# Moving the pooling work to other places in the queues of an attention loop

## The chip, the cores and the metric

The kernel runs on one core of a Trainium2 chip. The metric is device time in microseconds (us) of the whole program. The engines of the core are TensorE (PE in the profile; its weight loads are PEld), VectorE (DVE), ScalarE (ACT), GpSimd (POOL) and SyncE (SP, which issues most transfers). Each has its own queue of instructions, and they wait for each other through semaphores.

## The reference

The input is four images of 128 channels and 64 x 64 points. Layer 0 is a group norm, three 1x1 convolutions and full attention over the 4096 points of an image. Layer 1 takes the points as tokens. It has two parts, each with a residual addition: a causal attention with running maximum and running sums over 8 heads, and a sparse expert layer, which the change concerns:

```
logits = einsum('bsd,ed->bse', x, gate_w) + gate_b       # 64 experts
probs  = softmax(logits, axis=1)                          # over the 4096 tokens
vals, idx = top_k(probs.transpose(0, 2, 1), 8)            # 8 tokens for each expert
gathered  = take x at idx
pooled    = einsum('bked,bke->bed', gathered, topv)       # weighted sum of those 8
out       = two dense layers per expert on pooled
outputs[idx] += out * topv
```

"Pooling" below is the way from the logits to `pooled`: for every expert find the eight largest logits among 4096 tokens, take their probabilities, set all others to zero, and multiply by the tokens.

## The kernel before

Layer 0 fills the first 1500 us or so. Then comes the loop over 32 blocks n of 512 tokens (8 blocks for each of the four images; function `loop`, L977 to L1037), in which attention runs one block ahead of the gate, and after it the experts.

In a block PE works in this order, which is written out by hand (`manual_schedule` for PE, L1039): the keys of block n + 1 for the first four heads (`pk`, L687), the turned exponentials of block n (`pe`, L769), the turned gate tokens (`gtr`, L888), the keys of the other four heads, the values (`pv`, L805), the gate's logits (`pl`, L896), the turned tokens of block n + 2 (`ltr`, L677), the totals (`pt`, L821), the scores of block n + 1 (`ps`, L706) and the outputs (`po`, L841 and L848). Most of these results go through one ring of three PSUM buffers (tag `kv`). So a matmul into it waits until the result of three places before has been read: a key by its Silu on ScalarE (`ks`, L689), a value by its Silu (`v`, L809), `gtr` and `ltr` by copies on ScalarE (L890, L679).

The scores go through `scan`: VectorE makes a running maximum (`mm`, L723) and a difference (`ss`, L727); ScalarE takes its Exp (L728); VectorE makes running sums (`rr`, L738) and their reciprocal (L743); GpSimd copies the exponentials (`es`, L733). `spread` sends `rr` through memory to all partitions (`rb`, L751 and L758), and `weighted` multiplies `em` by `rb` on VectorE (L793). The scan of block n + 1 is written in block n, ahead of `outputs`.

Pooling of the first two images (group p = 0) is woven into the loop. With k0 = n - 18:

- `select(0)`, in block 18: finds the eight largest of the candidates (`cand`, eight for each 512 tokens) and marks the rest so that they match nothing.
- `pick(0, k0)`, in blocks 18 to 25: the **mark** (L927, VectorE) writes `left`, a copy of 512 logits with the chosen ones replaced by the lowest number; the **Exp** (L930, ScalarE) overwrites the logits with their exponentials and sums them up; the **choice** (L933, VectorE) keeps those whose place in `left` is the lowest number and sets the rest to zero.
- `pick_turn(0, k0 - 1)`, in blocks 19 to 26: four transposes (`ctr`, L940, between the keys and the values) and a multiplication (`ct`, L943, VectorE).
- `pick_add(0, k0 - 1)`, in the same blocks: 32 small matmuls (`pp`, L955, between the logits and `ltr`) and an addition (L967).
- `divisors(0)`, in block 26: sums and a reciprocal.

The two other images (p = 1) go through the same functions after the loop.

On engines other than PE, a planner sorts the instructions by their place in the program and by when it reckons their data to be ready. `tc.issue_after(i)` around some code adds an edge: instructions of that code on the engine of i come later in the queue than i. Before the change the pooling of block n is written behind `scan(n + 1)` with two such edges:

```
made = scan(n + 1, score(n + 1, ks))
rbs = spread(n + 1, made[1])
with tc.issue_after(made[2][0]), tc.issue_after(made[2][1]):
    if k0 == 0:
        select(0)
    if 0 <= k0 < NBLK:
        pick(0, k0)
```

`made[2][0]` is the scan's Exp and `made[2][1]` the reciprocal. So pooling's Exp is behind the scan's Exp, and mark and choice are behind the reciprocal.

ScalarE loads a table whenever it goes over from one of Exp, Silu and Sqrt to another (ACT_TABLE_LOAD in the profile; the gate's norm has a Sqrt, L90).

Of the kernel before, what the change touches and what calls it, by code (L numbers as in the profile page):

```python
# [8 lines left out]
F32 = mybir.dt.float32  # L9
AF = mybir.ActivationFunctionType  # L10
ALU = mybir.AluOpType
AX = mybir.AxisListType
PSUM = bass.MemoryType.PSUM
P = 128
LOWEST = -3.4028234663852886e38
# [3 lines left out]
def conv_attn_hybrid_kernel(  # L19
# [22 lines left out]
    nc = tc.nc  # L42
# [7 lines left out]
    BLK = 512  # L50
    NBLK = N // BLK
# [258 lines left out]
    with ExitStack() as l0:  # L310
# [36 lines left out]
        aas = load("aas", [P, 1], (every[:1], aa.to_broadcast([P, 1])))  # L347
# [289 lines left out]
    def layer1(pre, ready):  # L637

        with ExitStack() as kept, ExitStack() as l1:
            pool = opener(kept, pre)  # L640
            lgp = pool("lg", side="right")
            gp = pool("gate", side="right")
# [6 lines left out]
            ps_kv = pool("l1kv", 3, space=PSUM)  # L649
# [13 lines left out]
            def tokens(n):  # L663
# [6 lines left out]
                    made.append(xl)  # L670
                return made + [last]

            def turned(n, xls):

                ptr = ps_kv.tile([P, NPAIR, 2, 2, H2], F32, tag="kv", name=f"{pre}ltr_{n}")
                for c, xl in enumerate(xls[:CPB]):
                    nc.tensor.transpose(ptr[:, c // 2, :, c % 2, :], xl, ident)  # L677
                xt = sb.tile([P, BLK], F32, tag="xt", name=f"{pre}xt_{n}", bufs=3)
                nc.scalar.copy(xt, ptr.rearrange("p q s u j -> p (q s u j)"))  # L679
                return xt  # L680

            def keys(n, xt, heads):
# [19 lines left out]
            def score(n, ks):  # L702
                pss = ps_s.tile([P, BLK], F32, tag="s", name=f"{pre}ps_{n}")
                for h in range(NH):
                    g, r = h % QG, h // QG
                    nc.tensor.matmul(  # L706
                        pss[g * QW : (g + 1) * QW, :], qz[:, h, :], ks[h],
                        start=(r == 0), stop=(r == NR - 1),
                    )
                return pss  # L710
# [80 lines left out]
            def weighted(ems, rbs):  # L791
                for em, rb in zip(ems, rbs):
                    nc.vector.tensor_mul(em, em, rb.rearrange("p s h j -> p (s h) j"))  # L793
                return [em.rearrange("p (s h) j -> p s h j", s=2) for em in ems]
# [67 lines left out]
            rden = lgp.tile([P, B // 2], F32, tag="rden", name=f"{pre}rden")  # L862

            total = lgp.tile([P, B // 2, C + 1], F32, tag="total", name=f"{pre}total")
            gmv, grs, xgs, xts, picks, cts = {}, {}, {}, {}, {}, {}

            def gate_stats(n):
                gmv[n] = gp.tile([P, CPB, 2], F32, tag="gmv", name=f"{pre}gmv_{n}", bufs=2)
# [34 lines left out]
            def select(p):  # L903

                flat = cand[p].rearrange("p k e -> p (k e)")
                top = gp.tile([P, 8], F32, tag="top", name=f"{pre}top_{p}")
                nc.vector.max(out=top, in_=flat)
                ng = gp.tile([P, 1], F32, tag="ng", name=f"{pre}ng_{p}")
                nc.vector.tensor_scalar_mul(ng, top[:, 0:1], -1.0)
                sel = gp.tile([P, NBLK * 8], F32, tag="sel", name=f"{pre}sel_{p}")  # L910
                nc.vector.match_replace(
                    out=sel, in_to_replace=top, in_values=flat, imm_value=-LOWEST
                )
                nc.vector.tensor_scalar(
                    out=sel, in0=sel, scalar1=1e38, scalar2=None, op0=ALU.is_ge
                )
                nc.vector.tensor_mul(flat, flat, sel)
                nc.vector.tensor_scalar(
                    out=sel, in0=sel, scalar1=1.0, scalar2=3e38, op0=ALU.subtract, op1=ALU.mult
                )  # L920
                nc.vector.tensor_add(flat, flat, sel)
                picks[p] = ng

            def pick(p, k):
                lg = lgs[p][:, bass.ts(k, BLK)]
                left = gp.tile([P, BLK], F32, tag="left", name=f"{pre}left_{p}_{k}")
                nc.vector.match_replace(  # L927
                    out=left, in_to_replace=cand[p][:, k, :], in_values=lg, imm_value=LOWEST
                )
                nc.scalar.activation(  # L930
                    lg, lg, AF.Exp, bias=picks[p], accum_out=den[:, p, k : k + 1]
                )
                nc.vector.scalar_tensor_tensor(  # L933
                    out=lg, in0=left, scalar=-3.3e38, in1=lg, op0=ALU.is_le, op1=ALU.mult
                )

            def pick_turn(p, k, ps):
                ptr = ps.tile([P, CPB, P], F32, tag="kv", name=f"{pre}ctr_{p}_{k}")
                for c in range(CPB):
                    nc.tensor.transpose(ptr[:, c, :], lgs[p][:, bass.ts(k * CPB + c, P)], ident)  # L940
                ct = gp.tile([P, CPB, 2, E], F32, tag="ct", name=f"{pre}ct_{p}_{k}", bufs=2)
                rs = rs1[:, bass.ts(p, 2 * NCH)].rearrange("t (z i) -> t i z", z=2)
                i = nc.vector.tensor_mul(  # L943
                    ct, ptr.rearrange("t c (z e) -> t c z e", z=2),
                    rs[:, bass.ts(k, CPB), :].unsqueeze(3).to_broadcast([P, CPB, 2, E]),
                )
                cts[p, k] = ct
                return i.ins
# [20 lines left out]
            def divisors(p):  # L969
                nc.vector.tensor_reduce(rden[:, p : p + 1], den[:, p, :], AX.X, ALU.add)  # L970
                nc.vector.reciprocal(rden[:, p : p + 1], rden[:, p : p + 1])
# [5 lines left out]
            def loop():  # L977
                xt = {n: turned(n, tokens(n)) for n in range(2)}
                made = scan(0, score(0, keys(0, xt[0], range(NH))))
                rbs = spread(0, made[1])  # L980
                for n in range(NB):
                    more = n + 1 < NB
                    if more:
                        ks = keys(n + 1, xt[n + 1], range(NH // 2))
                    if n >= 1:
                        gate_stats(n - 1)
                    if not more:
                        gate_norm(n - 1, nc.vector)
                    if n + 2 < NB:
                        xls = tokens(n + 2)  # L990
                    if n == 0:
                        ks += keys(n + 1, xt[n + 1], range(NH // 2, NH))
                    es, rr, _ = made
                    ems = weights(n, es)
                    if n >= 2:
                        gate_turn(n - 2, ps_kv)
                    if more and n > 0:
                        ks += keys(n + 1, xt[n + 1], range(NH // 2, NH))
                    k0 = n - (B // 2 * NBLK + 2)
                    if 1 <= k0 <= NBLK:  # L1000
                        with tc.issue_after(pick_turn(0, k0 - 1, ps_kv)):
                            aas = weighted(ems, rbs)
                    else:
                        aas = weighted(ems, rbs)
                    vs, last = values(n, xt[n])
                    if n >= 2:
                        best = gate_logits(n - 2, ps_kv)
                    if not more:
                        gate_turn(n - 1, ps_kv)
                    if 1 <= k0 <= NBLK:  # L1010
                        pick_add(0, k0 - 1)
                    with tc.issue_after(last):
                        if n >= 1 and more:
                            gate_norm(n - 1, nc.gpsimd)
                        if n == 0 and ready:
                            roots(rs1[:, bass.ts(B - 1, NCH)], mv1[:, bass.ts(B - 1, NCH), :])
                    if n + 2 < NB:
                        xt[n + 2] = turned(n + 2, xls)
                    totals(n, vs)
                    if not more:  # L1020
                        best()
                        best = gate_logits(n - 1, ps_kv)
                    if more:
                        made = scan(n + 1, score(n + 1, ks))
                        rbs = spread(n + 1, made[1])
                        with tc.issue_after(made[2][0]), tc.issue_after(made[2][1]):
                            if k0 == 0:
                                select(0)
                            if 0 <= k0 < NBLK:
                                pick(0, k0)  # L1030
                            if k0 == NBLK:
                                divisors(0)
                    outputs(n, rr, aas, vs)
                    if n >= 2:
                        best()
                    if n == 0 and ready:
                        test_rows(gp, ps_kv)  # L1037
# [118 lines left out]
            for g in range(EG):  # L1156
# [5 lines left out]
                p, k = g // NBLK, g % NBLK  # L1162
# [100 lines left out]
```

## Time and profile before

| what | value |
|---|---|
| time, median of 3 | 2557.14 us (2555.38 to 2559.95) |
| span of the profiled execution | 2555.8 us |
| PE / DVE / ACT / POOL busy | 94% / 66% / 47% / 12% |
| the chain that ended last | PE 84%, DVE 9%, ACT 3%, DMA 2% |
| attention loop, first and last key or output matmul | 1501.4 to 2390.5 us |
| the scan's reciprocal (L743) | 32 times 3353 ns |
| mark (L927), Exp (L930), choice (L933) | 670, 722, 658 ns in the loop |
| table loads | 1283 ns each: 32 for the scan's Exp (L728), 40 for the keys' Silu (L689), 33 for the Sqrt (L90) |

The page's busy shares are means over stages of different kinds. What a change in one stage is worth has to be read from the blocks of that stage: how long a block is, how much of it PE is busy, and what ends PE's waits. The granted clock (PEclk) is the share of full speed at which PE ran. A wait for several semaphores is put down to the one that came last.

### The profile page before, as it was taken

How to read it: one execution, taken by the hardware profiler on the slowest of the kernel's cores; microseconds unless marked ns; L12 is line 12 of the kernel's file. 1: busy time of each engine (PE TensorE's matmuls, PEld its weight loads, DVE VectorE, ACT ScalarE, POOL GpSimd, SP SyncE). 2: the span in 40 equal slices, each digit the busy share in tenths (PEclk: the TensorE clock that was granted, in tenths of full speed). 3: DMA queues.
4: the chain of work that ended last, by engine and by line, in shares of the span. 5: the costliest groups of instructions: out<-in, count | busy, mean ns of one | idle time of the engine just before them, and what ended most of it. 6: DMA issues, size and time to landing. Idle time of an engine off the chain costs nothing.

```text
span 2555.8 us, 45522 instructions
## 1 busy us (share of the span) xinstructions
PE 2412.5 (94%) x19348; PEld 1598.9 (63%) x19348; DVE 1677.5 (66%) x2648; ACT 1206.8 (47%) x1575; POOL 310.0 (12%) x370
## 2 busy tenths in 40 slices
PE   5899999999999999999999989999999888899787
PEld 3567767677677677776777755555555454555543
DVE  6777777777776777766666656666666655566524
ACT  2344434444344444444444445666666555566341
POOL 0000000000000000000000003333333332333100
PEclk9999999999999999999999999999999889999898
DMA  3100110000100000000000001212212110112485
GB/s 97 54 17 16 26 47 9 17 13 22 50 13 5 21 17 17 17 9 9 5 9 5 5 18 35 52 38 49 51 36 52 35 35 19 34 36 51 157 330 209
DMA packets 48292, 111.03 MB, mean 43 GB/s; under 512 B 10192, under 2 KB 19024, under 8 KB 47952
## 3 DMA queue, kind: packets, MB, share of 16 engines
q1 hardware_dynamic: 46784, 107.77, 14.3%
q8 instruction: 153, 2.51, 0.4%
q14 instruction: 59, 0.48, 0.1%
q10 hardware_dynamic: 1296, 0.26, 0.1%
HBM read 86.38 MB, written 8.91 MB: 37 GB/s over the span
## 4 chain that ended last, share of the span: by engine, by line
PE 84%; DVE 9%; ACT 3%; DMA 2%; issue 1%; SPq 0%; ACTq 0%; DVEq 0%
PE av L494 33%; PE sc L470 17%; PE pv L805 8%; PE pk L687 8%; PE po L841 3%; PE pt L821 2%; DVE rr L743 2%; PE ps L706 1%; PE pa L437 1%; PE ph L1108 1%; PE pd L519 1%; DVE before L831 1%; PE pp L955 1%; PE pe L415 1%; PE pl L896 1%
## 5 line engine op out<-in xcount | busy, mean ns | idle before, releaser
L494 PE MATMUL av<-pr,am 64*128 64x512 f32 x4096 | 1189.6, 592 | 5.2 <-DVE o L505 5.2
L474 ACT ACTIVATE pr<-sc 128x1024 f32<-128x1024 f32 x512 | 523.9, 1023 | 704.4 <-PE sc L470 692.3
L494 PEld LDWEIGHTS av<-pr,am 64*128 64x128 f32 x4096 | 679.2, 188 | 257.9 <-issue 59.0
L481 DVE TENSOR_TENSOR acc<-acc,pr 128x1024 f32<-128x1024 f32 x480 | 585.5, 1220 | 332.3 <-ACT pr L474 320.2
L470 PE MATMUL sc<-e,e 64*128 64x512 f32 x2048 | 736.8, 594 | 0.0
L470 PEld LDWEIGHTS sc<-e,e 64*128 64x128 f32 x2048 | 351.7, 188 | 101.9 <-issue 28.8
L687 PE MATMUL pk<-xt,wks 128*128 128x512 f32 x512 | 252.3, 634 | 13.4 <-ACT ks L689 9.0
L805 PE MATMUL pv<-wvs,xt 128*128 128x512 f32 x512 | 227.7, 598 | 2.6 <-ACT v L809 2.6
L809 ACT ACTIVATE v<-pv 128x512 f32<-128x512 f32 x256 | 152.6, 597 | 71.4 <-PE pv L805 71.4
L687 PEld LDWEIGHTS pk<-xt,wks 128*128 128x128 f32 x512 | 96.2, 202 | 127.1 <-issue 81.4
L689 ACT ACTIVATE ks<-pk 128x512 f32<-128x512 f32 x256 | 146.8, 597 | 60.0 <-PE pk L687 59.6
L805 PEld LDWEIGHTS pv<-wvs,xt 128*128 128x128 f32 x512 | 97.4, 192 | 122.0 <-issue 115.4
L793 DVE TENSOR_TENSOR em<-em,rb 128x1024 f32<-128x1024 f32 x64 | 78.3, 1234 | 139.1 <-DMA rb<-rd 138.9
L695 POOL MEMSET ew<- 128x1024 f32 x1 | 1.0, 952 | 1050.6 <-PE pa L437 1050.6
L841 PEld LDWEIGHTS po<-v,em 64*64 64x64 f32 x4096 | 111.4, 133 | 26.7 <-DVE before L831 26.7
L95 POOL TENSOR_SCALAR xg<-t,gmv,grs 128x128 f32<-128x128 f32 x120 | 94.6, 801 | 237.4 <-DVE grs L91 122.8
L784 POOL TENSOR_TENSOR em<-et,mask 128x1024 f32<-128x1024 f32 x64 | 120.3, 1901 | 22.6 <-ACT et L771 22.6
L728 ACT ACT_TABLE_LOAD x32 | 41.1, 1283 | 169.5 <-DVE ss L727 169.5
L841 PE MATMUL po<-v,em 64*64 64x128 f32 x4096 | 119.2, 271 | 0.0
L527 DVE RECIPROCAL den<-den 128x512 f32<-128x512 f32 x32 | 107.3, 3353 | 1.1
L743 DVE RECIPROCAL rr<-rr 128x512 f32<-128x512 f32 x32 | 107.3, 3353 | 1.1
L729 POOL COPY state<-mm 128x1 f32<-128x1 f32 x32 | 20.6, 644 | 511.8 <-DVE mm L723 511.8
(164 smaller groups left out, 2319.1 us busy)
## 6 DMA issues: line engine op xcount, KB each, us to landing
rb<-rd SPq DMA_DIRECT2D x128, 256.0 KB
fw<-in_fw_dram SPq DMA_DIRECT2D x64, 512.0 KB
x<-in_x_dram SPq DMA_DIRECT2D x16, 512.0 KB
xr<-in_x_dram SPq DMA_DIRECT2D x32, 256.0 KB
e<-ee SPq DMA_DIRECT2D x64, 128.0 KB
out_dram<-t SPq DMA_DIRECT2D x16, 512.0 KB
e<-ee SPq DMA_DIRECT2D x64, 64.0 KB
rd<-rr SPq DMA_DIRECT2D x64, 8.0 KB
```

Of the source, the lines that this page charges most:

```text
L470: nc.tensor.matmul(sc[:, u, :], e2[halves[u], p, :], e1[halves[u], :], start=True, stop=True)
L474: nc.scalar.activation(pr, sc, AF.Exp)
L481: nc.vector.tensor_add(acc, acc, pr)
L494: nc.tensor.matmul(av, am[h, j, :], pr[h, u, :], start=(j == 0), stop=(j == NCH - 1))
L527: nc.vector.reciprocal(den, den)
L687: nc.tensor.matmul(pk, wks[:, h, :], xt, start=True, stop=True)
L689: nc.scalar.activation(ks, pk, AF.Silu)
L743: inverse = nc.vector.reciprocal(rr, rr).ins
L784: nc.gpsimd.tensor_tensor(em, eq.unsqueeze(2).to_broadcast([P, 2 * NH, H2]), mask.unsqueeze(1).to_broadcast([P, 2 * NH, H2]), ALU.mult,)
L805: nc.tensor.matmul(pv.rearrange("p h d -> p (h d)"), xt[:, bass.ts(2 * q + s, P)], wvs[:, bass.ts(m, BLK)], start=True, stop=True,)
L809: last = nc.scalar.activation(v[:, bass.ts(m, HPB), :], pv, AF.Silu).ins
L841: nc.tensor.matmul(po[s * H2 : (s + 1) * H2, u, q, :], aas[q][half, s, h, :], vs[2 * q + s][half, h, :], start=(q == 0 and h == 0), stop=F ...
```

## The change

Pooling's work stays the same; its places in the queues change.

- The mark of k0 goes into the first half of block n, ahead of the em multiplications (and in block 18 `select` goes in front of it, behind the reciprocal of that block's own scan).
- Pooling's Exp goes behind the xt copy of block n + 2 and in front of the scan's Exp in the second half of the same block, so that the two Exps stand side by side on ScalarE.
- The choice stays behind the reciprocal; its mark and Exp are now ahead of it.
- `divisors(0)` goes into the first half of block 26.

It is meant to take pooling's Exp, and VectorE's reciprocal ahead of its mark, out of the way of the keys' Silus at the start of a block.

```diff
-                nc.scalar.copy(xt, ptr.rearrange("p q s u j -> p (q s u j)"))
+                copied[n] = nc.scalar.copy(xt, ptr.rearrange("p q s u j -> p (q s u j)")).ins
...
             def pick(p, k):
-                lg = lgs[p][:, bass.ts(k, BLK)]
...
+                pick_mark(p, k)
+                pick_exp(p, k)
+                pick_keep(p, k)
...
                     k0 = n - (B // 2 * NBLK + 2)
-                    if 1 <= k0 <= NBLK:
-                        with tc.issue_after(pick_turn(0, k0 - 1, ps_kv)):
-                            aas = weighted(ems, rbs)
-                    else:
+                    with ExitStack() as order:
+                        if k0 == 0:
+                            with tc.issue_after(made[2][1]):
+                                order.enter_context(tc.issue_after(select(0)))
+                        if 0 <= k0 < NBLK:
+                            order.enter_context(tc.issue_after(pick_mark(0, k0)))
+                        if 1 <= k0 <= NBLK:
+                            order.enter_context(tc.issue_after(pick_turn(0, k0 - 1, ps_kv)))
+                        if k0 == NBLK:
+                            divisors(0)
                         aas = weighted(ems, rbs)
...
                     if more:
-                        made = scan(n + 1, score(n + 1, ks))
+                        pss = score(n + 1, ks)
+                        with ExitStack() as order:
+                            if 0 <= k0 < NBLK:
+                                with tc.issue_after(copied[n + 2]):
+                                    exp = pick_exp(0, k0)
+                                order.enter_context(tc.issue_after(exp))
+                            made = scan(n + 1, pss)
                         rbs = spread(n + 1, made[1])
-                        with tc.issue_after(made[2][0]), tc.issue_after(made[2][1]):
-                            if k0 == 0:
-                                select(0)
-                            if 0 <= k0 < NBLK:
-                                pick(0, k0)
-                            if k0 == NBLK:
-                                divisors(0)
+                        if 0 <= k0 < NBLK:
+                            with tc.issue_after(made[2][1]):
+                                pick_keep(0, k0)
```

`pick_mark`, `pick_exp` and `pick_keep` hold the three instructions of the old `pick`.

More of the change, by code (lines that the diff above doesn't have):

```diff
@@ L671, in tokens @@
                 return made + [last]
+            copied = {}
             def turned(n, xls):
@@ L864, in layer1 @@
             total = lgp.tile([P, B // 2, C + 1], F32, tag="total", name=f"{pre}total")
-            gmv, grs, xgs, xts, picks, cts = {}, {}, {}, {}, {}, {}
+            gmv, grs, xgs, xts, picks, cts, lefts = {}, {}, {}, {}, {}, {}, {}
             def gate_stats(n):
@@ L920, in select, with pick_mark, pick_exp, pick_keep @@
                 )
-                nc.vector.tensor_add(flat, flat, sel)
+                i = nc.vector.tensor_add(flat, flat, sel)
                 picks[p] = ng
-            def pick(p, k):
-                lg = lgs[p][:, bass.ts(k, BLK)]
[L926 to L930, printed above, removed]
+                return i.ins
+            def pick_mark(p, k):
+                left = gp.tile([P, BLK], F32, tag="left", name=f"{pre}left_{p}_{k}")
+                lefts[p, k] = left
+                i = nc.vector.match_replace(
+                    out=left, in_to_replace=cand[p][:, k, :], in_values=lgs[p][:, bass.ts(k, BLK)],
+                    imm_value=LOWEST,
+                )
+                return i.ins
+            def pick_exp(p, k):
+                lg = lgs[p][:, bass.ts(k, BLK)]
+                i = nc.scalar.activation(
                     lg, lg, AF.Exp, bias=picks[p], accum_out=den[:, p, k : k + 1]
                 )
+                return i.ins
+            def pick_keep(p, k):
+                lg = lgs[p][:, bass.ts(k, BLK)]
                 nc.vector.scalar_tensor_tensor(
-                    out=lg, in0=left, scalar=-3.3e38, in1=lg, op0=ALU.is_le, op1=ALU.mult
-                )
+                    out=lg, in0=lefts.pop((p, k)), scalar=-3.3e38, in1=lg,
+                    op0=ALU.is_le, op1=ALU.mult,
+                )
+            def pick(p, k):
+                pick_mark(p, k)
+                pick_exp(p, k)
+                pick_keep(p, k)
             def pick_turn(p, k, ps):
```

## The prediction

> **What bounds the kernel now.** I read the page first: TensorE (PE) is busy 94% of the span, and the chain that ended last is 84% PE. So a gain in the attention loop can only come from time in which PE stands still or runs slowly there. Block n of the loop ends with the last rr matmul of line 848, so the timeline cuts the loop into blocks, and the table of busy times by stretch shows them. Pooling touches blocks 18 to 26; its matmuls run in 19 to 26.
>
> ```profile
> core 0: us, PE busy (x) PEld busy (x) DVE busy (x) ACT busy (x) POOL busy (x), PEclk, DMA share, GB/s
> 1963.84:1988.79 24.95, 24.94 (x336) 14.16 (x335) 15.66 (x35) 15.96 (x26) 9.47 (x11) 1.00 0.19 45
> 1988.79:2025.31 36.52, 29.53 (x371) 16.85 (x371) 20.63 (x48) 19.41 (x31) 9.65 (x11) 0.91 0.13 31
> ...
> 2094.66:2128.97 34.31, 28.84 (x371) 17.23 (x371) 19.75 (x40) 19.43 (x30) 10.03 (x11) 0.90 0.14 33
> ...
> 2265.63:2290.31 24.68, 24.68 (x336) 14.23 (x335) 16.20 (x38) 15.84 (x25) 9.47 (x11) 1.00 0.17 45
> ```
>
> The rows are blocks 18, 19, 22 and 27: length, then busy time by engine, then the granted clock. A plain block is PE from end to end at clock 1.00; a pooling block is some 10 us longer, with PE idle for over 5 us of it and a clock of 0.90. Blocks 19 to 26 take 36.52, 34.85, 34.50, 34.31, 34.23, 34.01, 34.24 and 34.18 us, 276.84 together. The timeline of block 22 says where the idle time is:
>
> ```profile
> 2094.51 0.63 ACT L728 ACTIVATE ss<-ss 128x512 f32<-128x512 f32 x1
> ...
> 2096.90 3.35 DVE L743 RECIPROCAL rr<-rr 128x512 f32<-128x512 f32 x1
> 2097.07 1.28 ACT L930 ACT_TABLE_LOAD   x1
> ...
> 2100.19 0.67 DVE L927 MATCH_REPLACE8 left<-ca,lg 128x512 f32<-128x512 f32 x1
> ...
> 2100.89 0.72 ACT L930 ACTIVATE lg<-lg,ng 128x512 f32<-128x512 f32 x1 [2.54 <-DVE left L927]
> ...
> 2101.72 1.28 ACT L689 ACT_TABLE_LOAD   x1
> ...
> 2103.02 1.57 ACT L689 ACTIVATE ks<-pk 128x512 f32<-128x512 f32 x3
> ...
> 2103.76 1.09 PE L769 MATMUL pe<-ident,es 128*128 128x128 f32 x4 [5.47 <-ACT ks L689]
> ```
>
> Columns: start, duration, engine, line, and in brackets the idle time ahead and its releaser. The mark (L927) is queued behind the 3.35 us reciprocal, pooling's Exp (L930) waits for the mark, three Silus of the keys (L689) are queued behind that Exp and its table load plus one of their own, and PE waits for the PSUM buffers which those Silus empty. The table of waits for blocks 20 to 26 has it seven times:
>
> ```profile
> ACT L728 <- DVE ss L727: 44.9, 7, 6.4
> ...
> PE pe L769 <- ACT ks L689: 38.0, 7, 5.5
> ```
>
> 38.0 us in seven blocks; block 19 has 7.0 us more (it waits in front of the second half of the keys, with select also in its way). The first row is ScalarE's free time ahead of the scan's Exp, 6.4 us a block: the place to which the change moves pooling's Exp.
>
> **What the Trainium skill says.** "TensorE: Matmul & The Clock Gate", section "What's actually happening": PE falls to half clock after an idle window of about 3.4 us and needs about 3.4 us of work to come back. The trace agrees: behind the 5.47 us gap the four transposes of pe take 1.09 us, in block 28 0.60, and from pe to the first ctr transpose takes 6.35 us (2103.76 to 2110.11), where the same matmuls of plain block 28 take 4.39 (2294.05 to 2298.44). So a stall costs **1.96 us more** than its length. "ScalarE: Activation LUTs", "What ACT_TABLE_LOAD costs": 1.283 us for the load, and a drain of 1.38 on top. The load is 1.28 in every row here; no drain shows (scan Exp ends 2095.14, load, first Silu 2096.45: 1.31 in all), so I use 1.28. The same page, "Table sets: the hidden batching unit": copy and identity are in every set. Agrees: et, xt and lg have no load in front. "Perfetto Trace Analysis", "Tensor Engine Instruction (MATMUL, LD_WEIGHTS)", says ScalarE and VectorE are strict first-in, first-out; the ready Silus standing behind the waiting Exp above show it.
>
> **The change part by part**, from block 22 and plain blocks.
>
> 1. *Exp from behind the first Silus to in front of the scan's Exp.* Removes the stall: 5.47 us idle and 1.96 us slow clock in a block like 22. What must stay is pooling's PE work: ctr 0.44 us (2110.11 to 2110.55); pp, from pl start to ltr start 2.40 us (2117.42 to 2119.82) against 0.86 in block 28 (2305.30 to 2306.16), so 1.54; 0.06 between ltr and pt (0.59 against 0.53). Sum 2.04. Check: 24.67 (unstalled plain block) + 2.04 + 5.47 + 1.96 = 34.14 against 34.31.
> Does the Exp fit in its new place? The xt copy ends at 2121.11, ss is ready at 2127.43. Table load 1.28 + Exp 0.72 + accumulator read 0.19 = 2.19, so it ends near 2123.3, 4.1 us before the scan's Exp needs the engine. Behind it are only that Exp and the next keys' Silus. Cost: none.
> 2. *Two table loads fewer a block.* Pooling's Exp and the scan's share one, and a Silu load goes. Of 2.57 us saved on ScalarE, what matters is that the scan's Exp finds its table loaded: it starts at 2127.5, not 2128.83. The chain behind it (es, rr, rb, keys' Silus) is 1.28 us earlier. Plain blocks such as 28 lose some 0.28 us on the fourth key, because the first Silu ends too late to free its buffer (24.95 against 24.67). Pooling blocks should not: I take 24.67 for them.
> 3. *Mark before the em multiplications.* 0.67 us and its value load (0.03 to 0.09) on VectorE. In block 22 VectorE idles 3.65 us just before ct, in block 28 5.37 us before em while rb is on its way. Its data were made blocks ago, and its buffer left is freed by the previous choice, behind the reciprocal. Queued behind it: ct and em; em wait for rb anyway. Cost nothing, upper bound 0.76 us.
> 4. *Choice (L933) right behind the reciprocal.* 0.66 us. Its Exp is done long before. With the scan 1.28 us earlier, the block after 22 would start at 2128.97, its reciprocal end near 2133.3, the choice near 2133.9. PE reaches ctr 7.9 us into the block (keys 3.5, pe and gtr 0.88, keys 3.5), at 2136.9. Slack 3 us. The work behind it (residual add, statistics, ew) moves 0.66 us and is needed by totals, ten us later. Nothing.
> 5. *select into block 18.* Eight operations of 0.08 to 0.21 us, some 1.4 in all, in the 5 us ahead of em. Nothing. Block 18 stays at 24.95. divisors: two of 0.10 and 0.16 us, nothing.
>
> New pooling block: 24.67 + 2.04 = 26.71; eight of them 213.7 instead of 276.84: **63.1 us less**. The tail follows the loop: its weight loads are issued from 2391.39 on, behind the loop's last matmul at 2390.5, so it moves as a whole. 2557.14 - 63.1 = **2494.0**. With 24.95 for the plain part it is 2496.3.
>
> **Rivals.**
> - *The stall shrinks but stays* (13%). If the planner puts the choice behind residual add, copy, statistics and ew (0.68 + 0.22 + 1.22 + 1.99, the last with the slow ew copy of block 22), it ends at 2133.3 + 4.1 + 0.66 = 2138.1, and ctr waits 1.2 us; no clock is lost under 3.4 us. Eight times: 2494 + 9.6 = 2504; with the mark's 0.76 in front too, 2510. For it: VectorE's order is the planner's. Against: the choice is written ahead of the outputs that hold the residual add.
> - *The low clock belongs to pooling, not to the idle time* (2%). Then the blocks keep 0.90: 213.7 / 0.9 = 237.4, so 2518. Against: plain blocks have PE 100% busy at 1.00.
> - *The wait moves into the scan* (5%). The mark comes so late that pooling's Exp holds the scan's Exp, and with it the Silus, es and rb. The stall of 7.43 us then comes back in nine blocks, since the first mark and Exp now lie in block 18: 2494 + 9 x 7.43 + about 2 for select = **2563, slower than before**. For it: the scan's Exp is now ordered behind an operation that waits on VectorE. Against: the mark stands ahead of em, which ended at 2113.7 in block 22, some 7 us before the xt copy. If it returns only in part, the time is near that of before.
>
> **How the numbers follow.** Forecast 80%: 2490 to 2499, from 2494.0, 2496.3 and the spread of the times of before (2555.4 to 2560.0). Low end 2489. The upper end goes to the whole of the first rival, 2510; the last two stay out. Faster 95%: forecast, first and second rival. Of the third, 2% the same, 3% slower.
>
> **What would show it.** Pooling blocks of 26.7 us with clock 1.00; no wait of pe for ks; ScalarE's loads at L728 down from 32 to 24 and at L689 from 40 to 32; pooling's Exp done 4 us before the scan's, with no wait for left in the loop. Step 4 is wrong if ctr waits for the choice; step 1 if the scan's Exp waits for pooling's; the whole if a new PE gap over 3 us with a clock near 0.9 shows in blocks 18 to 26.

## The result, and the profile after

The changed kernel takes 2495.41 us (median of 4, 2493.74 to 2496.11) against 2556.51 us (median of 4) for the kernel before; the ratio is 0.9758, 95% interval 0.9741 to 0.9775. The prediction was 2494.0, range 2489 to 2510.

The table of busy times by stretch, for blocks 18, 19, 21 and 27 (length, busy time of PE, PEld, DVE, ACT and POOL, granted clock, DMA):

```profile
core 0: us, PE busy (x) PEld busy (x) DVE busy (x) ACT busy (x) POOL busy (x), PEclk, DMA share, GB/s
1964.50:1989.45 24.95, 24.95 (x336) 14.16 (x335) 21.53 (x46) 18.17 (x30) 10.25 (x13) 1.00 0.18 45
1989.45:2016.16 26.71, 26.71 (x371) 15.99 (x371) 18.25 (x41) 17.03 (x28) 9.68 (x12) 1.00 0.18 42
2069.61:2096.33 26.72, 26.72 (x371) 16.10 (x371) 18.20 (x41) 16.98 (x28) 9.62 (x12) 1.00 0.17 42
...
2203.21:2227.88 24.67, 24.67 (x335) 14.22 (x335) 15.89 (x35) 15.82 (x25) 9.47 (x11) 1.00 0.17 46
```

A pooling block is now PE from end to end, at clock 1.00. All eight take 26.71 or 26.72 us, 213.76 together instead of 276.84. On the page, PE's share of the chain that ended last has gone from 84% to 92%, and eight loads of Exp's table are gone from the scan's line:

```profile
PE 92%; DVE 4%; DMA 1%; ACT 1%; issue 1%; SPq 0%; ACTq 0%; DVEq 0%
...
L730 ACT ACT_TABLE_LOAD x24 | 30.8, 1283 | 118.9 <-DVE ss L729 118.9
```

The keys' Silu (now L691) loads its table 32 times instead of 40. The timeline of block 21 shows the new places (start, duration, engine, line; in brackets the idle time ahead and its releaser):

```profile
2070.70 0.60 ACT L691 ACTIVATE ks<-pk 128x512 f32<-128x512 f32 x1 [0.59 <-PE pk L689]
...
2073.07 0.60 PE L771 MATMUL pe<-ident,es 128*128 128x128 f32 x4
...
2073.84 0.63 DVE L946 SCALAR_TENSOR_TENSOR lg<-left,lg 128x512 f32<-128x512 f32 x1
...
2074.58 0.68 DVE L931 MATCH_REPLACE8 left<-ca,lg 128x512 f32<-128x512 f32 x1
...
2077.46 0.60 PE L959 MATMUL ctr<-ident,lg 128*128 128x128 f32 x4
...
2088.47 1.28 ACT L939 ACT_TABLE_LOAD   x1
...
2089.77 0.72 ACT L939 ACTIVATE lg<-lg,ng 128x512 f32<-128x512 f32 x1
...
2094.90 0.63 ACT L730 ACTIVATE ss<-ss 128x512 f32<-128x512 f32 x1 [4.32 <-POOL state L731]
```

The first Silu waits for PE and not PE for it; pe has no bracket; the choice is over 3 us before ctr reads it; pooling's Exp stands in ScalarE's free time, and 4.32 us of that time are left in front of the scan's Exp (ss itself is ready at 2094.78, so the copy that the bracket names is not what it waited for alone).

Where the time went, by stage, from the two profiles:

| stage | before | after | difference |
|---|---|---|---|
| start to the end of block 18 | 1988.79 | 1989.45 | +0.66 |
| blocks 19 to 26 | 276.84 | 213.76 | -63.08 |
| blocks 27 to 31 | 124.86 | 122.91 | -1.95 |
| behind the loop | 165.3 | 165.6 | +0.3 |

The third row is all in block 31 (25.78 against 23.83 us), where PE stands still for some 5 us in either kernel. How much slow clock follows differs from run to run: in experiments 1 to 6 below, which change nothing in that block, it takes 23.8 to 25.8 us.

### The profile page after: what moved, and what is told of

It reads as the page before. It is cut to its first block, busy times and chain, and to the rows that moved or that the text cites. A ratio compares the mean times of both kernels' runs of the same rounds, so it can differ in the third digit from the quotient of the medians.

```text
span 2491.7 us, 45505 instructions
## 1 busy us (share of the span) xinstructions
PE 2394.7 (96%) x19348; PEld 1590.2 (64%) x19348; DVE 1669.0 (67%) x2648; ACT 1187.5 (48%) x1559; POOL 306.3 (12%) x370
## 4 chain that ended last, share of the span: by engine, by line
PE 92%; DVE 4%; DMA 1%; ACT 1%; issue 1%; SPq 0%; ACTq 0%; DVEq 0%
PE av L494 34%; PE sc L470 17%; PE pk L689 9%; PE pv L807 9%; PE po L843 4%; PE pt L823 2%; PE ps L708 2%; PE pa L437 1%; PE ph L1135 1%; PE po L850 1%; PE pl L898 1%; PE pd L519 1%; PE pp L974 1%; PE pe L415 1%; DMA x<-in_x_dram 1%; PE po L1162 1%
## 5 line engine op out<-in xcount | busy, mean ns | idle before, releaser
L689 PE MATMUL pk<-xt,wks 128*128 128x512 f32 x512 | 241.9, 612 | 6.3 <-DVE inside L623 4.2
L691 ACT ACTIVATE ks<-pk 128x512 f32<-128x512 f32 x256 | 148.6, 597 | 60.8 <-PE pk L689 60.5
```

Source lines behind the costliest of these rows:

```text
L689: nc.tensor.matmul(pk, wks[:, h, :], xt, start=True, stop=True)
L691: nc.scalar.activation(ks, pk, AF.Silu)
```

## The experiments

The theory: PE stood still because the Silus that empty its PSUM ring stood behind pooling's Exp, and the slow clock followed from that. The rivals put it all down to the mark's wait, or all to the Exp's place, or the clock to pooling itself. Block lengths are cut at the last matmul of the outputs, as in the prediction.

**1. The mark alone.**

```diff
-  with tc.issue_after(copied[n + 2]): exp = pick_exp(0, k0)      # ahead of scan(n + 1)
+  made = scan(n + 1, score(n + 1, ks))
+  with tc.issue_after(made[2][0]), tc.issue_after(made[2][1]):
+      pick_exp(0, k0); pick_keep(0, k0)
```

> The mark stands early, as in the changed kernel; pooling's Exp and choice are again written behind the scan, and in the queue the Exp then stands between the scan's Exp and the keys' Silus. Theory (what counts is ScalarE's time ahead of the first Silu that frees a PSUM buffer): the scan's Exp loads its own table again (1.28 us later than in the changed kernel) and pooling's Exp with its read adds 0.91; 1.4 us of slack take most of it, and PE waits about 0.75 us on the fourth key: pooling blocks of 27.5 us, clock 1.00, 2495.4 + 8 x 0.75 = 2501. Rival 1 (the mark's wait behind the reciprocal was all of it): 26.7 us and 2495. Rival 2 (the Exp's place in front of the scan's Exp is all of it): the old blocks of 34.3 us and 2556.

Measured: 2499.15 us (2498.1 to 2501.96), ratio to the kernel before 0.9774 (0.9759 to 0.9789). Pooling blocks mostly of 27.36 us, 219.2 in all. From the timeline of the block that starts at 2097.64:

```profile
2097.48 0.63 ACT L730 ACTIVATE ss<-ss 128x512 f32<-128x512 f32 x1
...
2098.02 0.70 ACT L939 ACTIVATE lg<-lg,ng 128x512 f32<-128x512 f32 x1
...
2098.84 1.28 ACT L691 ACT_TABLE_LOAD   x1
...
2100.13 1.57 ACT L691 ACTIVATE ks<-pk 128x512 f32<-128x512 f32 x3
2100.78 1.13 PE L689 MATMUL pk<-xt,wks 128*128 128x512 f32 x2 [0.37 <-ACT ks L691]
```

Pooling's Exp waits for nothing and pushes the first Silu back; the fourth key waits for it. The lost time is 0.64 us a block (27.36 against 26.72), expected 0.75; 0.37 of it shows as idle time of PE. So an early mark alone brings most of the gain, given that the planner then also puts the Exp beside the scan's.

**2. The Exp back behind the first Silu, with the early mark.**

```diff
+  ks = keys(n + 1, xt[n + 1], range(1))
+  with tc.issue_after(silus[n + 1, 0]): exp = pick_exp(0, k1)       # k1 = k0 - 1
+  with tc.issue_after(made[2][1]): pick_keep(0, k1)
+  with tc.issue_after(exp): ks += keys(n + 1, xt[n + 1], range(1, NH // 2))
```

> The mark stands early, but pooling's Exp is put where it was before the change: behind the first Silu of the next block's keys. It waits for nothing; two table loads come back around it. Theory: the second Silu, which frees the buffer of pe, ends about 6.7 us into the block (scan's Exp 0.8, load 1.28, Silu 0.6, load 1.28, Exp and read 0.91, load 1.28, Silu 0.6), PE gets there at 3.8: a stall of 3.0 us plus 0.28 on the fourth key: blocks of 30.0 us, 2495.4 + 8 x 3.3 = 2521; if the clock falls for a stall of 3.0 us, up to 1.96 more each, 2537. Rival 1 (the mark's wait was all of it): 26.7 us, 2495. Rival 2 (only the place counts, not the wait): 34.3 us, 2556.

Measured: 2535.02 us (2534.79 to 2535.09), ratio 0.9912 (0.9896 to 0.9927). Blocks of 29.84 to 32.78 us, 252.6 in all. The timeline of block 22 has the stall, and the table of stretches the clocks of blocks 21 and 22:

```profile
2095.10 1.57 ACT L691 ACTIVATE ks<-pk 128x512 f32<-128x512 f32 x3
2095.84 0.63 PE L771 MATMUL pe<-ident,es 128*128 128x128 f32 x4 [2.92 <-ACT ks L691]
```

```profile
2057.57:2089.29 31.72, 28.79 (x371) 17.14 (x371) 19.20 (x40) 19.44 (x30) 9.99 (x11) 0.95 0.15 36
2089.29:2119.13 29.84, 26.91 (x371) 15.90 (x371) 19.27 (x40) 19.32 (x30) 10.00 (x11) 1.00 0.15 38
```

The stall is 2.92 us, expected 3.0, and block 22 with its 29.84 us is the one that keeps its clock. The other seven stall for 2.87 to 3.00 us and lose 1.4 to 2.9 us more. Neither rival's number is near. With experiment 1 this splits the 63.1 us of the eight blocks: 24.2 for the wait behind the reciprocal and the clock that it costs (276.84 to 252.6), 33.4 for taking the Exp out from between the Silus (to 219.2), 5.5 for putting it in front of the scan's Exp (to 213.76). The split holds for this order of the steps; the slow clock doesn't grow evenly with the stall, so in another order the shares can differ.

**3. The kernel before, with PE kept busy in its stall.**

```diff
+  if 2 <= k0 <= NBLK:                                   # ahead of weights(n, es)
+      warm = ps_s.tile([P, BLK], F32, tag="s", name=f"{pre}warm_{n}")
+      for i in range(6): nc.tensor.matmul(warm, ident, xt[n + 1], start=True, stop=True)
```

> The kernel before, with six 128x512 matmuls of no use put on PE in front of pe in blocks 20 to 26, where it stalls for 5.4 us; each takes 0.86 us, 5.2 in all, and writes a score buffer that is free then. Nothing else is changed. Theory (the slow clock follows the idle time and costs 1.96 us a block): seven blocks of 34.3 - 1.96 = 32.3 us at clock 1.00, 2556.5 - 13.7 = 2543. Rival (the low clock belongs to pooling's own work, or the stall costs only its length): blocks of 34.3 us or a little more, 2556.

Measured: 2543.36 us (2540.35 to 2547.78), ratio 0.9946 (0.9931 to 0.9961). The rows are block 19, which got no such matmuls, and block 22:

```profile
1991.27:2027.70 36.43, 29.45 (x371) 16.86 (x371) 20.63 (x48) 19.32 (x30) 9.66 (x11) 0.91 0.13 31
...
2092.47:2124.85 32.38, 32.06 (x383) 18.17 (x383) 19.75 (x40) 19.32 (x30) 10.03 (x11) 1.00 0.15 35
```

PE has 5.2 us more work and the block is 1.9 us shorter, since the clock stays at 1.00. The slow clock belongs to the idle time; the prediction's second rival falls.

**4. Six and sixteen further Exps in the new place.**

```diff
   exp = pick_exp(0, k0)
+  for i in range(6):                                    # 16 in the second kernel
+      again = sb.tile([P, BLK], F32, tag="again", bufs=1)
+      with tc.issue_after(exp): exp = nc.scalar.activation(again, lefts[0, k0], AF.Exp).ins
```

> The changed kernel with six further Exps of 512 columns (of no use) between pooling's Exp and the scan's Exp in blocks 18 to 25. In the changed kernel ScalarE is free for 4.3 us there. Theory (the Exp costs nothing because it fits into that free time): each takes some 0.49 us behind another, 3.1 in all, so the scan's Exp starts when it did: blocks of 26.7 us, 2495. Rival (work in front of the scan's Exp delays the scan and so PE, free time or not): 3.1 us less some 1 us of slack in each block, 28.8 us, 2512.

> The same with sixteen further Exps, 8.0 us in all, 3.7 more than there is room. Theory: the scan's Exp and the keys' first Silu come 3.7 us later; the fourth key waits for that Silu, which ends at 2.25 us after PE gets there: blocks of 29.0 us at clock 1.00, 2495.4 + 8 x 2.25 = 2513. With the clock lost in some blocks up to 2529. Rival (the scan's Exp has more slack than that, since PE needs its results only in the next block): 26.7 us, 2495.

Measured: 2491.74 us with six (2 runs, ratio 0.9742, 0.9724 to 0.976), 2554.56 us with sixteen (ratio 0.9987, 0.998 to 0.9994). With six, all eight blocks have 26.72 us. A block and its added Exps:

```profile
2068.54:2095.26 26.72, 26.72 (x372) 15.99 (x371) 18.20 (x41) 20.66 (x34) 9.64 (x12) 1.00 0.18 42
```

```profile
2089.43 3.93 ACT L1057 ACTIVATE again<-left 128x512 f32<-128x512 f32 x6
```

With sixteen they have 33.8 to 34.9. The timeline with sixteen:

```profile
2119.06 10.54 ACT L1057 ACTIVATE again<-left 128x512 f32<-128x512 f32 x16
...
2122.66 0.69 DVE L729 TENSOR_TENSOR ss<-ss,mm 128x512 f32<-128x512 f32 x1
...
2129.51 0.61 ACT L730 ACTIVATE ss<-ss 128x512 f32<-128x512 f32 x1
...
2132.08 1.22 PE L689 MATMUL pk<-xt,wks 128*128 128x512 f32 x1 [4.38 <-ACT ks L691]
```

Each added Exp took 0.66 us, not the 0.49 expected, so the scan's Exp came 6.2 us behind its ready operand (2129.51 against 2123.35) and not 3.7. Of the 10.54 us, 4.4 had room, which agrees with the 4.32 us of free time. PE waited 4.38 us, so some 1.8 of the 6.2 were slack behind the scan's Exp. The clock fell too (0.90 in this block), so that a block lost 7.4 us: 4.4 of waiting and 3.0 of slow clock. So the third rival is a real danger. What stands in front of the scan's Exp was free at 3.9 us and cost about as much as the old stall at 10.5; nothing between was run. By an estimate from this run, PE begins to wait at some 6 us (4.4 of room and 1.8 of slack).

**5. The shared table taken away.**

```diff
   exp = pick_exp(0, k0)
+  with tc.issue_after(exp): exp = nc.scalar.activation(other, ones, AF.Silu).ins      # one column
```

> The changed kernel with a one-column Silu between pooling's Exp and the scan's Exp in blocks 18 to 25, so that the scan's Exp has to load its table again behind the scan's difference. Theory (sharing the load is worth the 0.28 us by which the first Silu then misses the fourth key, as in the plain blocks of 24.95 us): pooling blocks of 27.0 us, 2495.4 + 8 x 0.28 = 2497.6. Rival (the load is hidden): 26.7 us, 2495.4.

Measured: 2493.39 us (2491.99 to 2494.41), ratio 0.975 (0.9735 to 0.9764). The load is back in the way of the scan's Exp and the block is no longer for it:

```profile
2094.00 1.28 ACT L730 ACT_TABLE_LOAD   x1 [2.79 <-DVE ss L729]
```

```profile
2095.43:2122.15 26.72, 26.72 (x372) 15.97 (x371) 17.87 (x40) 19.69 (x31) 9.62 (x11) 1.00 0.18 41
```

My expectation was wrong and the rival's right: seven of the eight pooling blocks have 26.72 us and one 26.85, so the shared load is worth nothing there.

**6. The load early in all blocks.** The same one-column Exp ahead of the scan's Exp in the blocks without pooling.

```diff
+  exp = nc.scalar.activation(first_exp, ones, AF.Exp).ins      # behind copied[n + 2], if not pooling
```

> The changed kernel, and in the blocks without pooling a one-column Exp stands where pooling's Exp stands in the others, so that Exp's table is loaded before the scan's Exp. Theory (the 0.28 us between blocks of 24.95 and 24.67 us is the first Silu held up by that load): blocks 11 to 18, 28 and 29 go to 24.67 us, 2495.4 - 10 x 0.28 = 2492.6. Rival (the 0.28 us has another cause): no block changes, 2495.4.

Measured: 2489.36 us (2488.98 to 2490.61), ratio 0.9734 (0.9721 to 0.9747). Blocks 11 to 18, 28 and 29 have 24.67 or 24.68 us. So in plain blocks the load does cost 0.28 us; the ten blocks make up 2.8 of the some 6 us to 2495.4, and block 30 another 0.3 (24.23 against 24.51). Block 1 gives 2.0 (28.32 against 30.30 us), which I had not expected. The one-column Exp stands in block 0 too, where it brings forward the scan's Exp and with it the reciprocal, behind which VectorE frees a buffer that PE waits for at the start of block 1. That wait, first in the changed kernel, then here:

```profile
1543.87 3.78 PE L689 MATMUL pk<-xt,wks 128*128 128x512 f32 x4 [4.21 <-DVE inside L623]
```

```profile
1542.16 3.45 PE L689 MATMUL pk<-xt,wks 128*128 128x512 f32 x4 [3.06 <-DVE inside L623]
```

The remaining 1 us or so is within the spread of the runs.

**7. Why the two kinds of block differ.** In the changed kernel VectorE's queue of plain block 14 has the candidates' maximum (MAX8) in front of the totals' additions, and waits for its input:

```profile
1857.96 0.69 DVE L903 MAX8 ca<-lg 64x8 f32<-64x512 f32 x1 [0.21 <-ACT lg L902]
1858.68 1.90 DVE L833 TENSOR_TENSOR before<-before,pt 128x128 f32<-128x128 f32 x6
```

PE began the totals at 1856.20, so the additions start 2.48 us behind it. In pooling block 21 PE begins at 2087.76, the maximum is over at 2088.75, and the additions start at 2089.85, 2.09 behind and waiting for PE alone. The run puts the maximum behind the reciprocal:

```diff
+  with tc.issue_after(made[2][1]):                      # if more
       best()
```

> The changed kernel with the candidates' maximum of a block (L903, 0.69 us on VectorE) behind the reciprocal instead of in front of the eight additions of totals and the scan. It is to say why the pooling blocks kept 26.72 us even with the scan's table load back in the way, while the plain blocks 11 to 18, 28 and 29 have 24.95 us. Theory: in plain blocks that maximum waits for the logits' copy on ScalarE (L902, behind the Sqrt's table load) and starts the additions, and with them the scan, some 0.3 us late; in pooling blocks PE spends 1.5 us on pooling in between, and the maximum is over by then. So plain blocks go to 24.67 us with the table load where it is, pooling blocks stay at 26.72: 2495.4 - 10 x 0.28 = 2492.6. Rival (the maximum has nothing to do with it, the table load alone has): all blocks as in the changed kernel, 2495.4.

Measured: 2490.2 us (2487.25 to 2490.68), ratio 0.9728 (0.9711 to 0.9746). Blocks 18 and 19:

```profile
1962.85:1987.52 24.67, 24.67 (x335) 14.22 (x335) 21.80 (x46) 18.00 (x29) 10.22 (x13) 1.00 0.18 45
1987.52:2014.24 26.72, 26.72 (x372) 15.99 (x371) 18.14 (x41) 16.99 (x28) 9.57 (x12) 1.00 0.16 42
```

All plain blocks with a scan behind them go to 24.67 us with the table load where it was. So the 0.28 us come only when both delays meet, the maximum's 0.39 (2.48 against 2.09) and the load's 1.28. By an estimate from these figures the chain has some 1.4 us of slack (0.39 + 1.28 - 0.28), which takes either delay alone; with sixteen added Exps the slack came out at some 1.8. In pooling blocks the maximum's delay is absent already, which fits experiment 5. The gain over 2495.4 is 5.2 us where 2.8 were expected; in the profile block 30 gives another 0.3 and block 31 another 0.7 (23.10 against 23.83), and the rest is within the spread of the runs.

**8. The same fault in block 1.** The test of layer 0's row sums puts one small result into the keys' PSUM ring at the end of block 0. VectorE reads it behind the reciprocal, and in the changed kernel PE waits 4.2 us for that buffer (3.1 in experiment 6, as the lines there show). On top of experiment 6 the test was moved behind the values of block 1:

```diff
   vs, last = values(n, xt[n])
+  if n == 1 and ready: test_rows(gp, ps_kv)
...
-  if n == 0 and ready: test_rows(gp, ps_kv)
```

> The version with the table loaded early in every block, and in it the test of layer 0's row sums (one small matmul into the PSUM ring of the keys, read by VectorE in line 623) goes from the end of block 0 to behind the values of block 1. Before, its result is read behind the reciprocal, and the second half of the first keys waits 4.2 us for that buffer. Theory (the same stall as pooling's: a buffer of the ring whose release stands behind the reciprocal, plus a slow clock): block 1 goes from 28.3 us (30.3 in the changed kernel) to some 23.7, 2489.4 less 4.6 to 6.6, 2484. Rival (block 1 is long because the pipeline starts up there, and the wait moves to another buffer): 28.3 us, 2489.

Measured: **2482.41 us** (2480.94 to 2485.62), ratio 0.9705 (0.9692 to 0.9718), the best of all. Block 1, first in the changed kernel, then here:

```profile
1537.52:1567.82 30.30, 26.09 (x331) 14.67 (x331) 18.92 (x35) 14.99 (x24) 10.34 (x11) 0.89 0.15 37
```

```profile
1539.45:1562.92 23.47, 23.47 (x332) 13.62 (x331) 15.59 (x36) 15.19 (x25) 10.58 (x12) 1.00 0.19 47
```

The wait is gone and has moved nowhere; 23.47 us against 23.7 expected. Against experiment 6 (28.32 us) that is 4.85 us of the 7 between the medians. Where the other 2 lie is open: the two profiles are 4.5 us apart in all, with block 31 1.9 us shorter here (23.84 against 25.77) and the time up to the end of block 0 2.5 us longer.

## Why the prediction was right, and where its steps were not

- **The bound and the stall (step 1): right.** 24.67 + 2.04 = 26.71 us was forecast for a pooling block, 26.72 is measured. Experiment 2 shows that Exp and table loads between the Silus were 2.92 us of the 5.47 us stall and the mark's wait the other 2.55; with both gone, the stall is gone. Experiment 3 shows that the slow clock is paid for the idle time. Its price of 1.96 us was read from one block, up to the ctr transposes; beyond their idle time the eight blocks lost 2.0 to 2.8 us against 26.72. The sum did not rest on it, since it sets the measured 276.84 us against eight new blocks. The free time left ahead of the scan's Exp was put at 4.1 us and is 4.32; experiment 4 finds 4.4.
- **Step 2: the number was right, its reason wrong.** The counts of loads came out (24 and 32), and pooling blocks do have 24.67 us for their plain part. But they have it with the load in the way too (experiment 5). I read the 0.28 us of plain blocks as the load's cost and did not look at what makes ss ready: there a maximum on VectorE starts the scan late, in pooling blocks it doesn't (experiment 7). The shared load is worth 0 there, not 0.28, so about 2.2 us of the forecast (eight times 0.28) came out right by luck.
- **Step 3: right in cost.** The mark takes 0.68 us. It stands right behind the choice and not in the idle time before em; the residual add gives way to it, and nothing waits for that.
- **Step 4: right.** The choice ends at 2074.47, ctr starts at 2077.46: 3.0 us of slack, as forecast.
- **Step 5: mis-sized, and hidden all the same.** select was put at 1.4 us and took 4.7, for a reason told below. em, which waits for rb, starts 13.1 us into block 18, and in plain block 28 of the kernel before at 13.25. Block 18 has its 24.95 us.
- **The first rival's "no clock is lost under 3.4 us": wrong,** and it didn't matter. In experiment 2, stalls of 2.87 to 3.00 us lost clock in seven blocks of eight. The Trainium skill, "TensorE: Matmul & The Clock Gate", section "What's actually happening", gives about 3.4 us of idle window; here less was enough, and the measurement decides. By the blocks of experiment 2, a wait of 3 us would have cost that rival up to twice its length. Whether the 1.2 us that it forecast cost clock, no run shows; waits of 0.3 to 0.4 us in experiment 1 did not (clock 1.00).
- **The sum.** 63.1 us were forecast for the blocks and 63.08 came. The tail moved as a whole (165.3 and 165.6 us). The medians are 61.1 us apart (2556.51 and 2495.41), and the forecast of 2494.0 is 1.4 us low. Where these 1.4 us lie is open; the runs of one kernel are 2.4 us (after) to 4.6 us (before) apart.

## What to carry to other kernels

When PE waits for a PSUM buffer, follow the buffer to the instruction that empties it, and then read what stands ahead of that instruction in its queue: one operation that waits there holds everything behind it. Such an operation belongs into the engine's own free time, ahead of a wait that exists anyway, and the free time has a size, which can be measured by filling it. A stall costs its length and, where the clock falls, the slow clock after it; filler work on PE tells the two apart.

## What the runs showed of the hardware that I had not expected

First, small VectorE operations became some nine to eleven times as long while GpSimd multiplied. From the changed kernel's block 18:

```profile
1972.19 0.21 DVE L913 MATCH_REPLACE8 sel<-top,ca 128x64 f32<-128x64 f32 x1
...
1972.55 3.75 POOL L786 TENSOR_TENSOR em<-et,mask 128x1024 f32<-128x1024 f32 x2
...
1972.67 1.86 DVE L919 TENSOR_TENSOR ca<-ca,sel 128x64 f32<-128x64 f32 x1
1974.56 1.79 DVE L920 TENSOR_SCALAR sel<-sel 128x64 f32<-128x64 f32 x1
1976.39 0.22 DVE L923 TENSOR_TENSOR ca<-ca,sel 128x64 f32<-128x64 f32 x1
```

The first of the two slow ones took 0.21 us in the kernel before, the second 0.16. GpSimd's two multiplications end at 1974.44 and 1976.30, the two slow operations at 1974.53 and 1976.35: each lasted until a multiplication was over. Other runs confirm it. In experiments 6 and 8, where `select` comes ahead of GpSimd's multiplications, these two took 0.22 and 0.19 us, and 0.23 and 0.20. In the kernel before, the first `ew` copy of blocks 19 to 26 begins just behind a multiplication's start and takes 1.9 us instead of 0.15 to 0.18; in experiment 2 it mostly begins 0.69 us into one and takes 1.25, so it again ends with it. Not every VectorE operation that overlaps is held: `ct`, with one input in PSUM, takes 0.69 us beside GpSimd's multiplications and without them. The Trainium skill, "GPSIMD Engine Reference", section "1. Specifications", names contention with GpSimd for VectorE instructions with two SBUF inputs or in a two-port mode. The trace agrees for the first kind (L919); in which mode the one-input operations ran, no run here shows.

Second, the slow clock after a stall had no single price, and a shorter stall could cost more. Beyond their idle time and the 26.72 us of an unstalled pooling block, blocks lost 2.0 to 2.8 us after stalls of 5.1 to 7.0 us (the kernel before), 2.4 to 3.0 after 4.4 to 5.8 (sixteen added Exps), and 0.2 to 3.1 after 2.9 to 3.0 (experiment 2). There the same instructions had PEclk 0.95 in block 21 and 1.00 in block 22.
